# The free-axis differences of a grid update: from turned matmuls to shifted sums on GpSimd and VectorE

## The chip, the cores and the metric

The kernel runs on one core of a Trainium2 chip. The core has a matrix engine (TensorE, PE in the profile, with its weight loads as PEld), a vector engine (VectorE, DVE), a scalar engine (ScalarE, ACT), GpSimd (POOL) and SyncE (SP), which here only issues DMAs. Each engine works through its own queue of instructions in order and waits on semaphores for the others. The metric is the device time of one execution in microseconds (us); less is better. Times shown are medians of several runs, and a profile is one further execution.

## What is computed

Sixteen samples of 256 x 256 go through four layers: an adapter with a layer norm, an attention block of 16 heads with a feed-forward part, a branch that is chosen per sample and has a layer norm, and at last one explicit step of a differential equation on the 256 x 256 field. The change is in the last layer:

```
def _L3_cond_ref(f, A_grid, B_grid, dt):
    def _grad(f, axis):
        fm = jnp.moveaxis(f, axis, -1)
        g = (jnp.roll(fm, -1, -1) - jnp.roll(fm, 1, -1)) * 0.5
        g0 = (-3.0 * fm[..., 0] + 4.0 * fm[..., 1] - fm[..., 2]) * 0.5
        gN = (3.0 * fm[..., -1] - 4.0 * fm[..., -2] + fm[..., -3]) * 0.5
        ...
    def _grad2(f, axis):
        g = jnp.roll(fm, -1, -1) - 2.0 * fm + jnp.roll(fm, 1, -1)
        g0 = 2.0 * fm[..., 0] - 5.0 * fm[..., 1] + 4.0 * fm[..., 2] - fm[..., 3]
        gN = 2.0 * fm[..., -1] - 5.0 * fm[..., -2] + 4.0 * fm[..., -3] - fm[..., -4]
        ...
    Af = A_grid[None] * f[:, None]
    Bf = B_grid[None] * f[:, None]
    gradv_Af = _grad(Af[:, 0], 1) + _grad(Af[:, 1], 2)
    gradvv_Bf = _grad2(Bf[:, 0], 1) + _grad2(Bf[:, 1], 2) + _grad(_grad(Bf[:, 2], 2), 1) + _grad(_grad(Bf[:, 2], 1), 2)
    df = -gradv_Af + gradvv_Bf * 0.5
    f_new = f + df * dt[:, None, None]
    return jnp.maximum(f_new, 0.0)
```

Axis 1 of a sample lies on the partitions (two chunks of 128), axis 2 is the free axis. With G for the first difference and H for half the second one, the update is G (b2 f G' - a0 f) + H (b0 f) + (H' on b1 f and -G' on a1 f along the free axis), where the primed ones work along axis 2 and a0, a1, b0, b1, b2 are the grids. G and H have one-sided rows at both ends.

## The kernel before

All four layers of all samples are in flight at once. Each stage is a Python generator, a chain: `adapt`, `prepare`, `project`, `weigh`, `attend`, `divide`, `enter`, `feed`, `end`, `step`. The class `Flow` puts the chains in an order when the program is built: it keeps a clock for each engine, adds a written-down cost for each piece of work (`flow.pe`, `flow.dve`, `flow.act`, `flow.pool`, `flow.dma`), and at each turn goes on with a chain that could start on PE by now, the one with the smallest priority number first. A `yield at` says from when a chain can go on, `yield at, 0` that it needs no PSUM bank, and a third element `True` that it goes ahead of the others. The priority of each chain starts at the first number in `flow.add(...)` and grows by the PE time it has used over the second. The order that comes out is fixed, and on the chip semaphores alone hold it together. Some choices hang on the clocks: `normalized` and `taken_up` take DVE or ACT for a layer norm's scaling and for a copy out of PSUM, and `feed` does so for its bias.

Attention takes 64 groups of four heads (`QUADS`, four per sample). For each, a side input of 1024 KB comes by SP (`load_side`, L332; three buffers), and a DMA issued from POOL (`add_mask`, L532) adds the mask to it in place. `weigh` emits this copy among its own instructions, by `MASK_FROM`, `MASK_BY` and POOL's clock. L841 on DVE then adds scores and side and takes the maximum, L852 on ACT makes the exponentials, four transposes (L479) turn them, `taken_up` (L487 on DVE, L489 on ACT) copies them to SBUF, and L908 multiplies them with the values. The layer norms' statistics go through four small POOL instructions each (L436 to L440).

`step` handles the last layer, one sample at a time. `normalized_affine` makes the field f (L448 or L453, then L471 and L472 on POOL). Then PE transposes f (tile e_t, four L479), and DVE makes three products of the turned field with turned grids (L1216: b2, a1, b1). POOL makes two products of f as it lies (L1220 b0, L1221 a0). PE forms b2 f G' in ps_z (L1228, L1229), DVE adds it to a0 (L1234). In ps_d, PE sums H and G along the partitions (L1246 for a chunk's own part, L1252 for the rows of the other chunk) and the free-axis differences of a1 and b1, which as turned fields are the stationary operands (L1262). One float32 matmul of the source stands as two instructions in the trace, and a transpose as one. DVE multiplies by dt and adds f (L1284), ACT takes the Relu (L1288), SP sends the result (L1290). `wide` gives the tiles of a step from eight buffers; a sample takes seven.

Of the kernel before, what the change touches and what calls it, by code (L numbers as in the profile page):

```python
# [98 lines left out]
class Flow:  # L99
# [63 lines left out]
    def run(self):  # L163
        while self.chains:
            open_ = [c for c in self.chains if c[4] is None or c[4]()]
            assert open_, "no chain can go on"
            now = self.clock["PE"] + 0.0774
# [19 lines left out]
def chain_kernel(ctx: ExitStack, tc: tile.TileContext, t: dict, out: bass.AP):  # L187
# [136 lines left out]
    sides, side_at, masked = {}, {}, {}  # L324
# [64 lines left out]
    def load_mask(b):  # L389
        m8s[b] = wp.tile([P, NC, S], U8, name=f"m8_{b}", tag="m8", bufs=1)  # L390
        nc.sync.dma_start(out=m8s[b], in_=t["mask"][b])
        if b:
            flow.dma(0.3)
# [13 lines left out]
    def later(name, src, shape, cost):  # L407
# [8 lines left out]
        later("rows_b", rows(t["rows_b"]), [P, 3 * D + B], 1.2),  # L416
# [6 lines left out]
    dt = rows_b[:, 3 * D :]  # L423
    w1_sr, w2_sr = w_sr[:, :NC, :], w_sr[:, NC:, :]
    a0_g, a1_g, b0_g, b1_g, b2_g, g_m, h_m = (grids[:, :, i * S : (i + 1) * S] for i in range(7))
# [17 lines left out]
    def normalized(dst, src, stat, first=False):  # L443
        mv, rs, nb = stat

        if first or max(flow.clock["DVE"], flow.clock["POOL"]) <= flow.clock["ACT"] - 0.2509:
            for c in range(NC):
                nc.vector.tensor_scalar(  # L448
                    dst[:, c, :], src[:, c, :], mv[:, c, 0:1], rs[:, c : c + 1], ALU.subtract, ALU.mult
                )  # L450
            return flow.dve(0.65, flow.clock["POOL"])
# [32 lines left out]
    def taken_up(dst, ps, after):  # L484

        if flow.clock["DVE"] + 0.9485 <= flow.clock["ACT"]:
            nc.vector.tensor_copy(dst, ps)  # L487
            return flow.dve(0.6, after)
# [165 lines left out]
    def project():  # L654
        for b in range(B):
# [6 lines left out]
            at = transposed(ps_t, ln)  # L662
            done.add(("turned", b))
# [117 lines left out]
    MASK_FROM, MASK_BY = 2, 1  # L781

    def weigh():

        at = 0.0
        for m, (b, half, par) in enumerate(QUADS):
# [43 lines left out]
            done.add(("scores", m))  # L830
            if masked[m] > flow.clock["DVE"]:
                yield max(at, masked[m]), 0
            for i in range(4):
# [32 lines left out]
                to = m + 2 if i >= MASK_FROM else m + 1  # L866
                if 4 <= to < len(QUADS) and to not in masked:
                    if to % 4 == 0 and to // 4 not in negs:
                        spread_mask(to // 4)
                    if to == m + 1 and i == MASK_BY or flow.clock["POOL"] > side_at[to]:  # L870
                        masked[to] = add_mask(to)
# [12 lines left out]
    def attend():  # L884
        for m, (b, half, par) in enumerate(QUADS):
            if m % 4 == 0:
                yield lambda: ("values", b) in done
            for i in range(4):
# [5 lines left out]
                at = transposed(ps_p, pr)  # L894
                p_t = hp.tile([P, NC, S], F32, name=f"c_pts{n}", tag="c_pts", bufs=4)
# [25 lines left out]
    def divide(b, half):  # L921
# [10 lines left out]
        for c in range(NC):  # L932
            nc.tensor.transpose(ps_r[:, c, :], spread[:, c].rearrange("p h d -> p (h d)"), ident)
        over = hp.tile([P, S], F32, name=f"c_over{b}_{half}", tag="c_over", bufs=1)
        nc.scalar.copy(over, ps_r.rearrange("p c q -> p (c q)"))
        at = free(f"c_r{b}_{half}", flow.act(0.29, flow.pe(0.22)))
# [36 lines left out]
    def enter():  # L973
        for b in range(B):
# [9 lines left out]
            at = transposed(ps_t, ln)  # L984
            h_t = hp.tile([P, NC, S], F32, name=f"d_ht{b}", tag="d_ht", bufs=2)
# [10 lines left out]
    def feed():  # L996
        for b in range(B):
# [6 lines left out]
            for j in range(NF // 2):  # L1004
# [16 lines left out]
                on_act = flow.clock["DVE"] > flow.clock["ACT"] - 0.4406  # L1021
# [79 lines left out]
    reach = [slice(0, P + 1), slice(P - 1, S)]  # L1101

    def end():
# [3 lines left out]
        for b in range(B):  # L1107
# [7 lines left out]
            at = transposed(ps_t, y)  # L1115
            x_t = wide(f"d_xt{b}")
# [64 lines left out]

    def step():
# [5 lines left out]
        def awake(*columns):  # L1188

            ps = misc("awake", [P, NC * S])  # L1190
            for n in columns:
                nc.tensor.matmul(ps[:, :n], ident, b2_g[:, 0, :n], start=True, stop=True)
            free("awake", flow.clock["PE"])

        yield lambda: ("branch", 0) in done
        for g in (a0_g, a1_g):
            nc.gpsimd.tensor_scalar(g, g, -1.0, None, ALU.mult)
        for b in range(B):
            yield lambda: ("branch", b) in done
            if b < B - 1:  # L1200
# [3 lines left out]
                yield at  # L1204
# [4 lines left out]
            at_f = at  # L1209
            ps_t = misc(f"e_t{b}", [P, NC, S])  # L1210
            at = transposed(ps_t, f)
            if b == B - 1:
                awake(256, 256)
            b2_, a1, b1_ = (wide(f"e_{n}{b}") for n in ("b2", "a1", "b1"))
            for dst, grid in ((b2_, b2_g), (a1, a1_g), (b1_, b1_g)):
                nc.vector.tensor_tensor(dst, ps_t, grid, ALU.mult)  # L1216
                at = flow.dve(0.6, at)
            free(f"e_t{b}", at)
            a0, b0 = wide(f"e_a0{b}"), wide(f"e_b0{b}")
            nc.gpsimd.tensor_tensor(b0, f, b0_g, ALU.mult)  # L1220
            nc.gpsimd.tensor_tensor(a0, f, a0_g, ALU.mult)  # L1221
            at_b = flow.pool(1.25, at_f)
            at_0 = flow.pool(1.25)
            yield at - 1.4
            ps_z = misc(f"e_z{b}", [P, NC, S])
            for c in range(NC):
                rng = slice(c * P, (c + 1) * P)
                nc.tensor.matmul(ps_z[:, c, :], b2_[:, 0, rng], g_m[:, 0, :], start=True, stop=False)  # L1228
                nc.tensor.matmul(  # L1229
                    ps_z[:, c, reach[1]], b2_[:, 1, rng], g_m[:, 1, reach[1]], start=False, stop=True  # L1230
                )
            at = flow.pe(1.39)
            yield at, 0, True
            nc.vector.tensor_tensor(a0, ps_z, a0, ALU.add)  # L1234
            at_z = free(f"e_z{b}", flow.dve(0.61, max(at, at_0)))
            yield at_b
            if b == B - 2:
                yield lambda: ("branch", B - 1) in done
            o = wide(f"e_o{b}")
            ps_d = misc(f"e_d{b}", [P, NC, S])  # L1240


# [15 lines left out]
            for c in range(NC):  # L1258
                rng = slice(c * P, (c + 1) * P)
                for k in range(NC):  # L1260
                    for src, w in ((a1, g_m), (b1_, h_m)):
                        nc.tensor.matmul(  # L1262
                            ps_d[:, c, reach[k]],
                            src[:, k, rng],
                            w[:, k, reach[k]],
                            start=False,
                            stop=False,
                        )
            flow.pe(2.74)
            yield at_z  # L1270
            for w, src in ((h_m, b0), (g_m, a0)):
                for c in range(NC):
                    next_to(w, src, c)
# [3 lines left out]
            yield at, 0, True  # L1277
# [5 lines left out]
            for part in [slice(c, c + 1) for c in range(NC)] if b == B - 1 else [slice(0, NC)]:  # L1283
                nc.vector.scalar_tensor_tensor(  # L1284
                    o[:, part, :], ps_d[:, part, :], dt[:, b : b + 1], f[:, part, :], ALU.mult, ALU.add
                )
                at = flow.dve(0.34 if b == B - 1 else 0.68, at)
                nc.scalar.activation(o[:, part, :], o[:, part, :], AF.Relu)  # L1288
                flow.dma(0.4 if b == B - 1 else 0.8, flow.act(0.54, at))
                nc.sync.dma_start(out=out[b].rearrange("(c p) d -> p c d", p=P)[:, part, :], in_=o[:, part, :])  # L1290
# [3 lines left out]
    flow.add(adapt(), -1.707, 2.551)  # L1294
    flow.add(prepare(), -2.177, 3.484)
    flow.add(project(), 1.419, 9.878)
    flow.add(weigh(), -3.911, 108.6)
    flow.add(attend(), 0.9418, 11.1)
    flow.add(enter(), -11.15, 0.3324)
    flow.add(feed(), 2.331, 13.51)  # L1300
    flow.add(end(), 12.69, 2.249)
    flow.add(step(), 2.08, 4.955)
    flow.run()

def _arrays(inputs):
# [28 lines left out]
    g, h = _stencils()  # L1334
    a_grid, b_grid = l3["A_grid"], l3["B_grid"]
# [55 lines left out]
```

## Time and profile before

| what | value |
|---|---|
| median of 3 runs | 889.37 us (887.1 to 889.7) |
| the profiled execution | 894.71 us |
| its span, first to last instruction | 892.5 us |
| mean granted clock of PE | 0.983 |
| DMA, mean share of 16 engines | 74%, 209 GB/s |
| last chain of waits, start to end | 871.0 to 889.6 us, nearly all PE work of the last two steps |
| side copies by SP, issue to landing, median | 6.3 us (63 of 1024 KB) |
| mask copies by POOL, issue to landing, median | 8.6 us (60) |

The profile gives for each engine the time in which it was busy. A busy PE is not always a full one: matmuls overlap, and the recorded time of one is longer than the distance to the next. In rows of groups the columns are line, engine, operation, output and inputs, shape and count, then busy time in us and the mean in ns, then idle time just before and what ended it. In a timeline the columns are start and duration in us, engine, line, operation, tiles, shape and count; consecutive like instructions are merged. In rows of stretches, each engine's busy time is followed by the count of its instructions, then come the granted PE clock, the DMA share and GB/s.

### The profile page before, as it was taken

What the parts mean: (1) busy time and instruction counts of PE and PEld (TensorE: products, weight loads), DVE (VectorE), ACT (ScalarE), POOL (GpSimd) and SP (SyncE); (2) the same over time, 40 slices, a digit from 0 to 9 for tenths busy, and PEclk for the clock granted to TensorE, in tenths of its full rate; (3) what the DMA queues carried; (4) which work ended last, traced back from release to release, by engine and by line L of the source; (5) the groups of instructions that cost most, each with busy time, mean ns of one, the idle gap of its engine ahead of it and who ended that gap; (6) DMA issues with size and microseconds to landing.
All of it is one profiled execution on the core that took longest, in us unless ns stands there. A gap on an engine that the chain in (4) does not pass through costs nothing. (4 is left out here: it accounts for less than half of the span.)

```text
span 892.5 us, 18369 instructions
## 1 busy us (share of the span) xinstructions
PE 844.9 (95%) x6188; PEld 663.9 (74%) x6188; DVE 598.5 (67%) x2034; ACT 572.5 (64%) x1616; POOL 377.9 (42%) x516
## 2 busy tenths in 40 slices
PE   7888999999999999899999999999998999999997
PEld 3565777777868777777778878777877778777875
DVE  5775977767666867666687768657757566665434
ACT  2686769678574867657477577658675665775320
POOL 3445653843544528154271625151513416131543
PEclk8998999999999999999899999999999999999999
DMA  7979999879776897967769696977786876940111
GB/s 274 363 226 275 231 308 264 230 207 276 200 221 168 252 248 187 265 157 223 203 183 268 165 311 206 257 200 220 225 215 198 226 204 184 270 108 13 59 43 36
DMA packets 79244, 186.84 MB, mean 209 GB/s; under 512 B 8473, under 2 KB 22699, under 8 KB 71083
## 3 DMA queue, kind: packets, MB, share of 16 engines
q1 hardware_dynamic: 46192, 120.51, 39.4%
q0 software_dynamic: 31680, 62.92, 33.1%
q10 hardware_dynamic: 1275, 2.19, 0.7%
q8 instruction: 52, 0.85, 0.4%
q14 instruction: 45, 0.37, 0.1%
HBM read 94.89 MB, written 4.19 MB: 111 GB/s over the span
## 5 line engine op out<-in xcount | busy, mean ns | idle before, releaser
L852 ACT ACTIVATE c_pr<-c_pr,c_mx 128x256 f32<-128x256 f32 x512 | 254.8, 500 | 97.8 <-DVE c_mx L841 96.5
L841 DVE CUSTOM_DVE_ANT_0 c_pr<-c_s,side 128x256 f32<-128x256 f32 x512 | 191.1, 417 | 47.9 <-PE c_pt L479 17.1
L479 PE MATMUL c_pt<-ident,c_pr 128*128 128x128 f32 x1024 | 144.6, 282 | 10.4 <-DVE c_mx L841 5.6
L479 PEld LDWEIGHTS c_pt<-ident,c_pr 128*128 128x128 f32 x1024 | 117.0, 143 | 39.3 <-issue 12.4
L532 POOL DMA_DIRECT2D side<-neg x60 | 80.1, 1342 | 127.7 <-DVE c_mx L841 74.0
L436 POOL TENSOR_SCALAR rs<-mv 128x2 f32<-128x2 f32 x64 | 14.2, 222 | 275.5 <-DVE mv L433 274.8
L1010 PE MATMUL d_f<-d_ht,w 128*128 128x256 f32 x512 | 125.8, 390 | 1.0 <-DVE c_mx L841 0.5
L1042 PE MATMUL d_o<-w,d_z 128*128 128x256 f32 x512 | 121.4, 382 | 0.3
L487 DVE COPY c_pts<-c_pt 128x512 f32<-128x512 f32 x124 | 84.0, 685 | 40.2 <-PE c_pt L479 38.3
L1010 PEld LDWEIGHTS d_f<-d_ht,w 128*128 128x128 f32 x512 | 95.9, 195 | 16.7 <-issue 2.4
L1042 PEld LDWEIGHTS d_o<-w,d_z 128*128 128x128 f32 x512 | 94.4, 191 | 13.9 <-issue 1.3
L489 ACT COPY c_pts<-c_pt 128x512 f32<-128x512 f32 x132 | 74.4, 574 | 40.5 <-PE c_pt L479 39.9
L852 ACT ACTIVATION_READ_ACCUMULATOR c_pr<-c_pr,c_mx 128x1 f32 x512 | 96.7, 189 | 0.0
L908 PE MATMUL c_c<-c_pts,c_va 128*32 128x256 f32 x1024 | 72.2, 385 | 3.4 <-DVE c_cts L940 2.9
L822 PE MATMUL c_s<-c_st 32*128 32x256 f32 x960 | 47.7, 305 | 6.4 <-PEq L1146 2.9
L822 PEld LDWEIGHTS c_s<-c_st 32*128 32x128 f32 x960 | 34.4, 185 | 25.4 <-issue 13.0
L908 PEld LDWEIGHTS c_c<-c_pts,c_va 128*32 128x32 f32 x1024 | 27.8, 109 | 31.6 <-issue 11.0
L1034 DVE SCALAR_TENSOR_TENSOR d_z<-d_f,d_z 128x512 f32<-128x512 f32 x64 | 43.5, 680 | 10.9 <-ACT d_f L1030 9.0
L437 POOL TENSOR_TENSOR rs<-rs,inv_sqrt 128x2 f32<-128x2 f32 x64 | 45.8, 716 | 5.3
L1030 ACT ACTIVATE d_f<-d_z 128x512 f32<-128x512 f32 x64 | 38.4, 601 | 12.4 <-DVE d_z L1027 10.8
L1027 DVE TENSOR_SCALAR d_z<-d_f,cols 128x256 f32<-128x256 f32 x82 | 35.7, 477 | 14.7 <-PE d_f L1010 14.2
L841 DVE DVE_READ_ACCUMULATOR2_ANT c_mx<- 128x1 f32 x512 | 42.5, 83 | 0.0
(166 smaller groups left out, 1522.6 us busy)
## 6 DMA issues: line engine op xcount, KB each, us to landing
side<-in_side SPq DMA_DIRECT2D x63, 1024.0 KB, 6.3
side<-neg POOLq DMA_DIRECT2D x60, 1024.0 KB, 8.6
c_st<-c_qk SPq DMA_DIRECT2D x60, 192.0 KB, 5.4
d_w<-in_W_branch SPq DMA_DIRECT2D x16, 512.0 KB, 5.7
c_st<-c_qk SPq DMA_DIRECT2D x60, 128.0 KB, 5.5
xt<-in_x_t SPq DMA_DIRECT2D x16, 256.0 KB, 7.2
x<-in_x SPq DMA_DIRECT2D x16, 256.0 KB, 4.8
c_st<-c_qk SPq DMA_DIRECT2D x60, 64.0 KB, 5.3
```

Of the source, the lines that this page charges most:

```text
L437: nc.gpsimd.tensor_tensor(rs, rs, inv_sqrt, ALU.pow)
L479: nc.tensor.transpose(ps[:, k, c * P : (c + 1) * P], src[:, c, k * P : (k + 1) * P], ident)
L487: nc.vector.tensor_copy(dst, ps)
L489: nc.scalar.copy(dst, ps)
L532: nc.gpsimd.dma_start(out=sides[m].rearrange("p (h c) k -> p h (c k)", h=HB), in_=negs[m // 4].rearrange("p c k -> p (c k)").unsqueeze(1). ...
L822: nc.tensor.matmul(ps[i][:, c, :], stacked[rows32, par, 0, c * P : (c + 1) * P], stacked[rows32, par, part, :], start=part == 1, stop=part ...
L841: nc.vector.tensor_tensor_reduce(out=pr[:, c, :], in0=ps[i][:, c, :], in1=sb[:, i * NC + c, :], scale=-1.0, scalar=3.0e38, op0=ALU.add, op ...
L852: nc.scalar.activation(pr[:, c, :], pr[:, c, :], AF.Exp, bias=mx[:, c : c + 1], scale=-1.0, accum_out=sums[:, c, h : h + 1],)
L908: nc.tensor.matmul(ps_c[32 * i : 32 * i + 32, :], va[:, k, 4 * half + i, 2 * par : 2 * par + 2, :].rearrange("p e d -> p (e d)"), turned[i ...
L1010: nc.tensor.matmul(ps_f[:, i, :], w1[:, k, f * P : (f + 1) * P], h_t[:, k, :], start=k == 0, stop=k == NC - 1,)
L1034: nc.vector.scalar_tensor_tensor(z, ps_f, 1.0, z, ALU.add, ALU.mult)
L1042: nc.tensor.matmul(ps_o, us[f // 2][:, f % 2, c * P : (c + 1) * P], w2[:, f, :], start=f == 0, stop=f == NF - 1,)
```

## The change

The free-axis differences are no longer made with a turned field. The transposes, ps_z and the sixteen L1262 instructions go. Five products are made of f as it lies: w = b2 f, a0, b0, p and q, where the grids for p and q are prepared once on POOL (p_g becomes half the difference of the two loaded grids, q_g half their sum, w_g half the b2 grid). Interior columns come from sums of tiles shifted by one column: r from p and q, and a0 gets w of the right neighbour and loses w of the left one. The two outer columns come from small products of the outer four columns with prepared edge coefficients. For samples 0 to 14, w is made on DVE and a0, b0, p, q and the three sums of r on POOL; for sample 15, w, a0 and the three sums are on DVE and b0, p, q on POOL. The output then is (ps_d + r) dt + f, in r's own buffer. ps_d keeps only the partition-axis parts.

```diff
+    def shifted(engine, clock, cost, r, p, q, at):
+        mid, left, right = (slice(i, i + S - 2) for i in (1, 0, 2))
+        engine.tensor_tensor(r[:, :, mid], p[:, :, right], p[:, :, mid], ALU.subtract)
+        engine.tensor_tensor(r[:, :, mid], r[:, :, mid], q[:, :, left], ALU.add)
+        engine.tensor_tensor(r[:, :, mid], r[:, :, mid], q[:, :, mid], ALU.subtract)
+        return clock(3 * cost, at)
...
-        yield lambda: ("branch", 0) in done
-        for g in (a0_g, a1_g):
-            nc.gpsimd.tensor_scalar(g, g, -1.0, None, ALU.mult)
+        yield lambda: ("finish", 0) in done
+        edge_r, edge_z, edge_t = (fixed(f"edge_{n}", edge) for n in "rzt")
+        for dst, grid, i in ((edge_r, p_g, 0), (edge_t, q_g, 1), (edge_z, w_g, 2)):
...
+            nc.gpsimd.tensor_tensor(dst, ends(grid), of.unsqueeze(1).to_broadcast(edge), ALU.mult)
+        nc.gpsimd.tensor_tensor(edge_r, edge_r, edge_t, ALU.add)
+        nc.gpsimd.tensor_scalar(a0_g, a0_g, -1.0, None, ALU.mult)
...
+        nc.gpsimd.tensor_tensor(diff, q_g, p_g, ALU.subtract)
+        nc.gpsimd.tensor_tensor(q_g, q_g, p_g, ALU.add)
+        nc.gpsimd.tensor_scalar(p_g, diff, 0.5, None, ALU.mult)
+        for g in (q_g, w_g):
+            nc.gpsimd.tensor_scalar(g, g, 0.5, None, ALU.mult)
...
-            ps_t = misc(f"e_t{b}", [P, NC, S])
-            at = transposed(ps_t, f)
-            for dst, grid in ((b2_, b2_g), (a1, a1_g), (b1_, b1_g)):
-                nc.vector.tensor_tensor(dst, ps_t, grid, ALU.mult)
-            nc.gpsimd.tensor_tensor(b0, f, b0_g, ALU.mult)
-            nc.gpsimd.tensor_tensor(a0, f, a0_g, ALU.mult)
-            ps_z = misc(f"e_z{b}", [P, NC, S])
...
-            nc.vector.tensor_tensor(a0, ps_z, a0, ALU.add)
+            if end_:
+                nc.vector.tensor_tensor(w, f, w_g, ALU.mult)
+                nc.vector.tensor_tensor(a0, f, a0_g, ALU.mult)
+                made = ((b0, b0_g), (p, p_g), (q, q_g))
+            else:
+                nc.vector.tensor_tensor(w, f, w_g, ALU.mult)
+                made = ((a0, a0_g), (b0, b0_g), (p, p_g), (q, q_g))
+            for dst, grid in made:
+                nc.gpsimd.tensor_tensor(dst, f, grid, ALU.mult)
+            if not end_:
+                at_r = shifted(nc.gpsimd, flow.pool, 1.25, r, p, q, at_q)
+            nc.vector.tensor_tensor(a0[:, :, mid], a0[:, :, mid], w[:, :, right], ALU.add)
+            nc.vector.tensor_tensor(a0[:, :, mid], a0[:, :, mid], w[:, :, left], ALU.subtract)
+            for i, g in enumerate((edge_z, edge_r)):
+                nc.vector.tensor_tensor(prod[:, i], ends(f), g, ALU.mult)
+            nc.vector.tensor_tensor(half, prod[:, :, :, :, 0:2], prod[:, :, :, :, 2:4], ALU.add)
+            for i, dst in enumerate((a0, r)):
+                nc.vector.tensor_tensor(outer(dst), half[:, i, :, :, 0], half[:, i, :, :, 1], ALU.add)
+            if end_:
+                at_r = shifted(nc.vector, flow.dve, 0.6, r, p, q, at_q)
...
-                    for src, w in ((a1, g_m), (b1_, h_m)):
-                        nc.tensor.matmul(ps_d[:, c, reach[k]], src[:, k, rng], w[:, k, reach[k]], ...)
...
-                nc.vector.scalar_tensor_tensor(o[...], ps_d[...], dt[:, b : b + 1], f[...], ALU.mult, ALU.add)
+                nc.vector.tensor_tensor(o, ps_d[:, part, :], o, ALU.add)
+                nc.vector.scalar_tensor_tensor(o, o, dt[:, b : b + 1], f[:, part, :], ALU.mult, ALU.add)
```

The host side gives the grids unturned and adds 24 numbers (the one-sided coefficients) to rows_b.

The rest of the change is in the plan. The mask copies get a chain of their own, in place of the lines in `weigh`:

```diff
+    def mask():
+        for m in range(4, len(QUADS)):
+            yield lambda: m in sides
+            if m % 4 == 0:
+                yield m8_at[m // 4], 0
+                spread_mask(m // 4)
+            yield side_at[m], 0, True
+            masked[m] = add_mask(m)
...
+            yield lambda: m in masked
```

After the transposes in `project`, `attend`, `enter` and `end`, and around the copies in `divide`, a `yield at, 0, True` is added, so that the copy out of PSUM is put in its place (and on its engine) only when the plan's clock has come to it. The plan's numbers are others: the allowance in `Flow.run` (0.0774 to 0.04507), the three thresholds of the engine choices (0.2509 to 0.354, 0.9485 to 0.5659, 0.4406 to 0.3293), and the start and rate of every chain.

## The prediction

> **What bounds the kernel now.** I read the page's first part for the engines' shares, then the busy time by stretches of the span, then the groups of instructions kept apart by shape, and last the timeline of a stretch without attention, to see whether a busy PE is a full one.
>
> ```profile
> PE 844.9 (95%) x6188; PEld 663.9 (74%) x6188; DVE 598.5 (67%) x2034; ACT 572.5 (64%) x1616; POOL 377.9 (42%) x516
> ```
>
> ```profile
> 89.00:178.00 89.00, 84.06 (x657) 65.28 (x656) 73.46 (x262) 66.82 (x202) 51.99 (x71) 1.00 0.93 260
> 803.00:848.00 45.00, 44.55 (x282) 37.23 (x277) 22.65 (x58) 20.52 (x49) 16.21 (x25) 1.00 0.11 36
> ```
>
> ```profile
> 808.29 0.60 PE L1228 MATMUL e_z<-grids,e_b 128*128 128x256 f32 x2
> 808.72 0.39 PE L1229 MATMUL e_z<-grids,e_b 128*128 128x129 f32 x2
> 808.95 0.60 PE L479 MATMUL c_pt<-ident,c_pr 128*128 128x128 f32 x4
> ...
> 810.25 0.39 PE L1262 MATMUL e_d<-grids,e_a 128*128 128x129 f32 x2
> 810.47 0.39 PE L1262 MATMUL e_d<-grids,e_b 128*128 128x129 f32 x2
> ```
>
> PE is busy for 844.9 of 892.5 us, so it idles for 47.6. From 803 to 848, with 11% DMA and DVE half idle, it is busy for 44.55 of 45.00 us, and the starts show that this is a full queue: two L1262 follow two others after 0.22 us, two 256-wide L1228 take 0.43, two L1229 0.23. So there one instruction costs 0.11 us (128 or 129 columns) or 0.215 (256), and its recorded 0.27 to 0.40 is overlap. From 89 to 178 the other engines are at their fullest (DVE 73.46 of 89, 83%; DMA 0.93) and PE still has 84.06. Every group of PE instructions, at the pitch of its starts (median), adds up to about 825 us. PE is the bound in nearly all stretches but the first 45 us and the last 20.
>
> [...]
>
> **What is removed on PE.** Per sample four transposes (0.44 us at 0.11), four 256-wide and four 129-wide instructions of ps_z (0.86 and 0.44), and sixteen L1262 (1.76): 28 instructions, 3.50 us, and 56.0 for 16 samples. They stand inside the full stream, so all of it counts. Two PSUM tiles per sample fall away too; an easier choice of bank may close holes, which I bound by 0 to 5 us and take as 0.
>
> **What moves to POOL.** Before, a sample has two multiplications there.
>
> ```profile
> L1220 POOL TENSOR_TENSOR e_b<-y,grids 128x512 f32<-128x512 f32 x16 | 22.9, 1428 | 1.3 <-DVE y L465 1.0
> L471 POOL TENSOR_TENSOR e_tmp<-e_tmp,rows_b 128x512 f32<-128x512 f32 x15 | 19.5, 1300 | 14.4 <-DVE e_tmp L448 13.6 <-ACT e_tmp L453 0.8
> ```
>
> After, samples 0 to 14 have four multiplications and three shifted sums, sample 15 three multiplications: 108 - 32 = 76 more, at 1.27 (the fastest of this size in the timeline) to 1.43: 97 to 109 us, taken 103. The preparation of the grids grows to about 10 us (four scalings at 1.56, two wide sums at 1.35, six small ones near 0.2), 7 more than now. POOL goes from 378 to 488. In the built instruction list it is a burst of seven, 7 x 1.27 = 8.9 us, and what queues behind it are the statistics of other samples (L436 to L440), for which ACT or DVE normalise and PE then transposes, and mask copies.
>
> **What DVE gets.** Out go three L1216 (0.685 each) and L1234 (0.69), 2.74 us. In come w (0.69), two 254-wide sums into a0 (0.68 each), five edge instructions (0.17 to 0.24 by the 128x16 rows at the start of the kernel, 0.2 taken) and the sum of ps_d and r (0.69 like L1234): 3.74. That is 1.0 per sample and 2.7 more for the last, whose a0 and shifts are on DVE: 19 us. The new plan also gives copies to other engines (built lists: c_pts on DVE 124 to 154, at 0.685; c_ln 24 to 14, d_z 82 to 72, d_ln 10 to 16, d_xt 4 to 6, e_tmp 26 to 24): DVE +14, ACT about -8 with two more table loads of 1.283. DVE stands at 631, ACT at 564. At a span near 848 that is 74% and 67%, under the 83% beside which PE stayed at 94%: the cover is DVE's idle time, and gone above 83%.
>
> **The new contact of DVE and POOL.** Nine of the new DVE instructions per sample (w, two sums, five edges, the last multiply-add) read only SBUF. The trace has few such rows; nearest are the normalisations L448, which read SBUF alone.
>
> ```profile
> 633.90 0.73 DVE L448 TENSOR_SCALAR e_tmp<-y,mv,rs 128x256 f32<-128x256 f32 x2
> ```
>
> ```profile
> 97.97 1.69 DVE L448 TENSOR_SCALAR c_ln<-x,mv,rs 128x256 f32<-128x256 f32 x2
> ```
>
> ```profile
> 97.40 1.77 POOL L544 TENSOR_TENSOR x<-x,rows_a 128x512 f32<-128x512 f32 x1
> ```
>
> A pair takes 0.73 alone and 1.69 here, ending soon after POOL's wide instruction; over the timeline the 12 pairs that overlap wide POOL work take 1.17 in the mean, 1.82 at most, the others 0.75. PSUM readers show nothing (L487 0.686 and 0.687). So one instruction pays 0 to 1.1 us, 0.21 in the mean, which I take: 9 x 15 x 0.21 = 28 us more DVE busy time, 659 or 78%, still covered. For its delay to others and for statistics behind the burst I put 6 us on the path, bounds 0 and 30.
>
> [...]
>
> **The rest.** Preparing the grids: 10 us of POOL behind sample 0's statistics, near 75 us, covered by PE work of samples 1 and 2; 2 us taken, bounds 0 and 10. The end: in the built PE list sample 15's feed-forward has little of other samples between its parts, so PE waits about 2.1 us for the last gate (0.84 + 0.60 + 0.69), 1.5 for the turned copy, 2.1 for the branch's Gelu with its table. Against this, L1174 no longer starts 2.3 us after its matmuls, behind sample 14's products. I take +4, bounds -2 and +8. Sample 15's own step stays near 10 us: two products, two sums and edges 3.8, shifts 2.05, then adds and Relu near 2.2, behind 1.4 for sample 14's output. rows_b grows from 392 to 404 KB, 0.06 us at 209 GB/s, under the early side loads. The mask chain issues the same 60 copies and 16 spreads at other places in POOL's queue; the late copies change order alone. Both are in the 6 us, with the mask's own risk below.
>
> **Sum.** 892.5 - 56.0 + 6 + 2 + 4 = 848.5 span. The profiled execution took 894.71, 2.2 around its span, so 850.7; the median shown, 889.37, is 0.6% below that execution (x 0.994): 845.5, said as 845.
>
> **Rivals.** First, late masks.
>
> ```profile
> DVE c_pr L841 <- DMA side<-neg: 8.7, 3, 5.8
> ```
>
> DVE waits for a mask three times now. Issue of L532 plus its median 8.6 us to landing, against the first L841 of each quad, leaves slacks of -0.4 to 18.5 us, 38 of 60 below a burst's 8.9. In the built list 12 bursts still have mask copies behind them. If each pushes one back by its 8.9 us, the mean lateness over these slacks is 2.15: 26 us, 874.5 span, 876.7 with what lies around it, median 871. For it: POOL's queue is in order. Against: only 6 of the 60 copies stand directly behind a burst, and PE has other chains to run.
>
> Second, the slower side: DVE becomes the bound through POOL's bursts. The place is the nine SBUF instructions of a step, the price 1.1 us each: 9 x 15 x 1.1 = 149, DVE 631 + 149 = 780, and at 82.5% fill the span is 945, median 942. It is slower than before from DVE 736 on (0.825 x 892.5), or 0.78 us an instruction. For it: bursts and these instructions belong to the same sample. Against: overlapping pairs pay 0.21.
>
> Third, no change: PE's place in the queue is taken by waits already there, and 889 stays. The full stretch from 803 to 848 speaks against it.
>
> Fourth, the full gain and closed holes: 892.5 - 61 = 831.5, median 829 or less.
>
> **Chances.** The forecast (828 to 862) 0.66, late masks 0.14, DVE bound 0.07, no change 0.03, better than 828 0.10. The range 826 to 868 takes the first, about half of the last and half of the masks: 0.78 to 0.80. A difference of 0.3% is about what the measurement can tell from none: faster 0.90, same 0.03, slower 0.07.
>
> **What would show it.** PE busy near 789 with 448 fewer instructions, idle near 60; DVE 645 to 675; POOL near 490, its new wide sums at 1.3 to 1.45; DVE's 254-wide sums near 0.9 where they meet POOL. Mask waits of DVE above 30 us would show the first rival, DVE above 730 the second. I am wrong if PE idles for over 80 us, or if idle falls below 45.

## The result and the profile after

The changed kernel takes 938.63 us (936.89 to 942.14, four runs), against 888.24 us (885.52 to 889.70) for the kernel before on the same chip: a ratio of 1.0576, interval 1.0533 to 1.0619. Forecast were 845 us, with 0.07 for a slower kernel. The profiled execution has a span of 935.9 us and a mean granted clock of 0.927, against 892.5 and 0.983.

The page's first part, and from its slices the row of the granted clock, for the kernel after:

```profile
PE 828.3 (89%) x5740; PEld 620.8 (66%) x5740; DVE 697.1 (74%) x2135; ACT 566.2 (60%) x1602; POOL 492.3 (53%) x602
...
PEclk8999999999899998997997989998899979899886
```

The 448 PE instructions are gone (5740 against 6188), and POOL has 492.3 us where 488 was worked out. Yet PE's busy time fell by 16.6 us only, and it idles for 107.6 us (935.9 - 828.3) instead of 47.6. The forecast had 789 busy and about 60 idle, so 39 us of the 87 by which the span missed are instructions that ran longer, and 48 are idle time. The granted clock says why they ran longer: 13 of the 40 slices lie below 0.9. In steps of 2.5 us, the time with a granted clock under 0.75 is 133 us; before it was 35. PE's busy time in each of these steps, times the part of the clock that is missing there, adds up to 50 us, and before to 14: the difference of 36 us is nearly all of the 39.

The list of waits, first for the kernel after, then before. A row has who waited, for whom, us in total, how often, and the longest; rows of other waits stand between these.

```profile
ACT c_pr L861 <- DVE c_mx L850: 161.8, 106, 11.9
...
PEld e_d L1296 <- DVE e_a L1279: 25.1, 10, 5.4
DVE e_r L1279 <- POOL e_r L1194: 21.1, 9, 2.5
```

```profile
ACT c_pr L852 <- DVE c_mx L841: 96.5, 89, 4.0
```

ACT's exponentials wait 65 us longer for the maxima that DVE takes, and the longest wait has gone from 4.0 to 11.9 us. L850 itself is as fast as before (416 ns). So it starts late, behind something in DVE's queue. The groups of the step on DVE by line and shape, kernel after, show behind what; then two of POOL:

```profile
L1273 DVE TENSOR_TENSOR e_a<-e_a,e_w 128x508 f32<-128x508 f32 x16 | 30.9, 1930 | 8.7 <-POOL e_a L1266 8.5
L1261 DVE TENSOR_TENSOR e_w<-y,grids 128x512 f32<-128x512 f32 x15 | 28.3, 1889 | 5.5 <-POOL y L471 5.5
L1274 DVE TENSOR_TENSOR e_a<-e_a,e_w 128x508 f32<-128x508 f32 x16 | 23.3, 1455 | 0.6
L1276 DVE TENSOR_TENSOR e_ed<-y,edge_z 128x16 f32<-128x16 f32 x16 | 15.2, 949 | 0.0
L1317 DVE SCALAR_TENSOR_TENSOR e_r<-e_r,rows_b,y 128x512 f32<-128x512 f32 x15 | 11.8, 785 | 0.5
L1277 DVE TENSOR_TENSOR e_eh<-e_ed 128x16 f32<-128x16 f32 x16 | 10.2, 637 | 0.6
L1316 DVE TENSOR_TENSOR e_r<-e_d,e_r 128x512 f32<-128x512 f32 x15 | 10.1, 677 | 7.6 <-PE e_d L1290 7.6
```

```profile
L1266 POOL TENSOR_TENSOR e_p<-y,grids 128x512 f32<-128x512 f32 x16 | 27.6, 1726 | 0.0
L1266 POOL TENSOR_TENSOR e_q<-y,grids 128x512 f32<-128x512 f32 x16 | 27.4, 1713 | 0.0
```

L1316, which reads PSUM, has the expected 0.68 us. Five of the rows that read only SBUF (w, the two sums into a0, the first edge product L1276, the edge sum L1277) have two to six times their own time, a 16-column product 0.95 us in the mean. The means hide the shape: the fifteen products w took 0.66 to 1.50 us twelve times and 4.79, 5.61 and 6.88 us three times. The timeline of the longest:

```profile
480.06 1.34 POOL L531 DMA_DIRECT2D side<-neg  x1
...
480.95 1.75 POOL L1266 TENSOR_TENSOR e_a<-y,grids 128x512 f32<-128x512 f32 x1
481.01 6.88 DVE L1261 TENSOR_TENSOR e_w<-y,grids 128x512 f32<-128x512 f32 x1
482.20 1.73 POOL L1266 TENSOR_TENSOR e_b<-y,grids 128x512 f32<-128x512 f32 x1
483.42 1.72 POOL L1266 TENSOR_TENSOR e_p<-y,grids 128x512 f32<-128x512 f32 x1
484.64 1.71 POOL L1266 TENSOR_TENSOR e_q<-y,grids 128x512 f32<-128x512 f32 x1
485.86 1.48 POOL L1192 TENSOR_TENSOR e_r<-e_p 128x508 f32<-128x508 f32 x1
487.41 1.60 POOL L1193 TENSOR_TENSOR e_r<-e_r,e_q 128x508 f32<-128x508 f32 x1
...
488.09 0.40 ACT L933 COPY c_spr<-c_rec 128x256 f32<-128x256 f32 x1 [6.17 <-DVE c_rec L931]
...
488.90 0.66 PE L937 MATMUL c_r<-ident,c_spr 128*128 128x128 f32 x2 [5.29 <-DVE c_qk L732]
```

POOL's product begins 0.06 us ahead of DVE's. The next POOL instructions start every 1.22 us although each is recorded with 1.7: five in a row follow without a pause. The first pause comes when the fifth ends (485.86 + 1.48 = 487.34), as L1193 needs its result; w ends at 487.89, 0.55 us later, a little less than its own 0.66 us. Nothing else runs on DVE in this time; ACT then has waited 6.17 us and PE 5.29. Not every burst holds DVE for so long. In another one of this kernel the same products are in the queue, and DVE gets in between them:

```profile
236.29 1.26 POOL L1266 TENSOR_TENSOR e_b<-y,grids 128x512 f32<-128x512 f32 x1
236.35 1.74 DVE L1273 TENSOR_TENSOR e_a<-e_a,e_w 128x508 f32<-128x508 f32 x1 [0.64 <-POOL e_a L1266]
237.51 1.71 POOL L1266 TENSOR_TENSOR e_p<-y,grids 128x512 f32<-128x512 f32 x1
238.13 1.64 DVE L1274 TENSOR_TENSOR e_a<-e_a,e_w 128x508 f32<-128x508 f32 x1
239.19 1.70 POOL L1266 TENSOR_TENSOR e_q<-y,grids 128x512 f32<-128x512 f32 x1
```

The sum waits for the product that is running, about 1.1 us, and POOL's q starts 1.68 us after p instead of 1.22. What tells the two kinds apart is what POOL did just before. Six of the fifteen bursts start 0.9 us after POOL issued a mask copy (L531, at 480.06 above). In these six all four products are recorded with 1.71 to 1.79 us and start 1.22 to 1.25 us apart, and there lie all five instructions of the step that took over 2 us: the three long w and two sums of 5.16 us. In the nine other bursts no instruction paid more than about 1.1 us. Why a burst behind a mask copy lets nothing in is not shown, and no run moved the mask copies away.

The stretch of the long w in busy times per 5 us (PE, PEld, DVE, ACT, POOL, each with its count, then the granted clock, DMA share and GB/s):

```profile
480.00:485.00 5.00, 3.61 (x40) 2.33 (x32) 4.68 (x5) 1.92 (x7) 5.00 (x6) 1.00 0.98 270
485.00:490.00 5.00, 1.10 (x5) 0.80 (x6) 5.00 (x9) 1.28 (x4) 4.84 (x5) 0.88 0.40 100
490.00:495.00 5.00, 3.41 (x11) 2.10 (x9) 4.90 (x15) 1.48 (x6) 3.08 (x3) 0.50 0.87 228
495.00:500.00 5.00, 5.00 (x18) 2.94 (x18) 1.85 (x8) 2.03 (x8) 0.00 (x0) 0.50 1.04 288
```

PE runs dry, and after that its granted clock is 0.50 for 10 us. What that makes of the same work, four transposes, before the burst and after it:

```profile
475.12 0.60 PE L478 MATMUL d_t<-ident,y 128*128 128x128 f32 x4
...
499.01 1.06 PE L478 MATMUL c_pt<-ident,c_pr 128*128 128x128 f32 x4
```

The clock of 0.50 came after the 5.29 us in which PE stood still; how short a gap brings it is not shown.

### The profile page after: what moved, and what is told of

Read it like the earlier page. It is cut to its first block, busy times and chain, and to the rows that moved or that the text cites. A ratio compares the mean times of both kernels' runs of the same rounds, so it can differ in the third digit from the quotient of the medians.

```text
span 935.9 us, 17580 instructions
## 1 busy us (share of the span) xinstructions
PE 828.3 (89%) x5740; PEld 620.8 (66%) x5740; DVE 697.1 (74%) x2135; ACT 566.2 (60%) x1602; POOL 492.3 (53%) x602
## 5 line engine op out<-in xcount | busy, mean ns | idle before, releaser
L861 ACT ACTIVATE c_pr<-c_pr,c_mx 128x256 f32<-128x256 f32 x512 | 255.0, 499 | 163.1 <-DVE c_mx L850 161.8
L850 DVE CUSTOM_DVE_ANT_0 c_pr<-c_s,side 128x256 f32<-128x256 f32 x512 | 192.5, 416 | 26.2 <-PE c_s L830 8.9
L478 PE MATMUL c_pt<-ident,c_pr 128*128 128x128 f32 x1024 | 161.2, 285 | 7.7 <-DVE c_mx L850 2.0
L478 PEld LDWEIGHTS c_pt<-ident,c_pr 128*128 128x128 f32 x1024 | 119.1, 144 | 52.5 <-issue 20.9
L531 POOL DMA_DIRECT2D side<-neg x60 | 80.3, 1346 | 89.9 <-DMA side<-in_side 30.1
L1017 PE MATMUL d_f<-d_ht,w 128*128 128x256 f32 x512 | 123.2, 385 | 4.7 <-ACT d_ht L994 2.5
L486 DVE COPY c_pts<-c_pt 128x512 f32<-128x512 f32 x154 | 104.9, 684 | 29.5 <-PE c_pt L478 28.4
L1017 PEld LDWEIGHTS d_f<-d_ht,w 128*128 128x128 f32 x512 | 93.6, 192 | 18.2 <-ACT d_ht L994 2.9
L912 PE MATMUL c_c<-c_pts,c_va 128*32 128x256 f32 x1024 | 75.8, 395 | 10.0 <-DVE c_pts L486 5.7
L488 ACT COPY c_pts<-c_pt 128x512 f32<-128x512 f32 x102 | 57.8, 575 | 19.5 <-PE c_pt L478 18.7
L912 PEld LDWEIGHTS c_c<-c_pts,c_va 128*32 128x32 f32 x1024 | 28.7, 110 | 43.4 <-issue 16.6
L830 PE MATMUL c_s<-c_st 32*128 32x256 f32 x960 | 49.6, 311 | 2.0 <-DVE c_pts L486 1.0
L850 DVE DVE_READ_ACCUMULATOR2_ANT c_mx<- 128x1 f32 x512 | 42.3, 83 | 0.0
L1034 DVE TENSOR_SCALAR d_z<-d_f,cols 128x256 f32<-128x256 f32 x72 | 31.4, 478 | 9.7 <-PE d_f L1017 9.5
```

The source lines that it names most:

```text
L478: nc.tensor.transpose(ps[:, k, c * P : (c + 1) * P], src[:, c, k * P : (k + 1) * P], ident)
L488: nc.scalar.copy(dst, ps)
L531: nc.gpsimd.dma_start(out=sides[m].rearrange("p (h c) k -> p h (c k)", h=HB), in_=negs[m // 4].rearrange("p c k -> p (c k)").unsqueeze(1). ...
L830: nc.tensor.matmul(ps[i][:, c, :], stacked[rows32, par, 0, c * P : (c + 1) * P], stacked[rows32, par, part, :], start=part == 1, stop=part ...
L850: nc.vector.tensor_tensor_reduce(out=pr[:, c, :], in0=ps[i][:, c, :], in1=sb[:, i * NC + c, :], scale=-1.0, scalar=3.0e38, op0=ALU.add, op ...
L861: nc.scalar.activation(pr[:, c, :], pr[:, c, :], AF.Exp, bias=mx[:, c : c + 1], scale=-1.0, accum_out=sums[:, c, h : h + 1],)
```

## The experiments

Theories. A: a DVE instruction that reads only SBUF is held while POOL's burst reads SBUF, DVE's queue stops behind it, PE idles and its clock falls. B: the plan's changes do it. C: the burst's length does it, as masks and statistics queue behind it on POOL. D: DVE's queue stands still in order, in front of an instruction that needs POOL's result.

**1. The plan alone.** Against the changed kernel, as all diffs here but those of runs 9 and 11, which name theirs: the step of the kernel before, with the mask chain, the late copies, the allowance and the thresholds of the change; the chains' starts and rates are those of before.

```diff
-        yield lambda: ("finish", 0) in done
-        edge_r, edge_z, edge_t = (fixed(f"edge_{n}", edge) for n in "rzt")
...
+            ps_t = misc(f"e_t{b}", [P, NC, S])
+            at = transposed(ps_t, f)
...
-    flow.add(step(), 0.9776, 1.725)
+    flow.add(step(), 2.08, 4.955)
```

> The step of before (turned field) under the new plan's mask chain, late copies and thresholds, with the old rates of the chains. Theory A (DVE instructions that read only SBUF are held by POOL's burst, stop DVE's queue, PE idles and its clock falls): 880 to 900 us, PE clock 0.97 or more. Theory B (the plan's changes cost the time): 920 or more.

899.91 us, ratio 1.0112 (1.0082 to 1.0143), clock 0.982. This part of the plan costs about 1% on the old step, far from the 920 us of B. The chains' new starts and rates are not in it; run 2 has the new step without any of the plan.

**2. The new step alone**, under the whole plan of before.

```diff
-            now = self.clock["PE"] + 0.04507
+            now = self.clock["PE"] + 0.0774
...
-            yield lambda: m in masked
...
+                    if to == m + 1 and i == MASK_BY or flow.clock["POOL"] > side_at[to]:
+                        masked[to] = add_mask(to)
...
-    flow.add(step(), 0.9776, 1.725)
+    flow.add(step(), 2.08, 4.955)
```

> The new step under the whole old plan. Theory A: 920 to 955 us, clock near 0.93, the w product on DVE again up to several us long. Theory B: 830 to 860, since the step alone saves 56 us of PE work.

981.93 us, 1.1005 (1.0895 to 1.1115), clock 0.92; w has a mean of 1.61 us, the two sums 1.82 and 1.54, and ACT waits 174 us for the maxima. More than either theory gave, and with run 1 it rules B out as the cause: with the new step, the new plan is worth some 43 us (981.9 - 938.6).

**3. DVE's part behind the burst.**

```diff
-                nc.vector.tensor_tensor(w, f, w_g, ALU.mult)
-                at_w = flow.dve(0.6, at)
...
                 at_r = shifted(nc.gpsimd, flow.pool, 1.25, r, p, q, at_q)
+                yield at_r + 2.0, 0
+                nc.vector.tensor_tensor(w, f, w_g, ALU.mult)
+                at_w = flow.dve(0.6)
```

> The changed kernel, but for samples 0 to 14 the DVE part of a step is put into the plan after POOL's seven instructions by the plan's clock. Theory A: DVE's w near 0.7 us in most samples, clock 0.96 or more, 850 to 890 us. Theory C (POOL's burst itself holds masks and statistics back): stays at 925 to 945, since POOL's work is the same. Theory B: stays too.

892.63 us, 1.0042 (1.002 to 1.0064), clock 0.962. POOL's burst has the same work, and 46 us have come back, so the burst by itself doesn't explain most of the loss. But DVE now waits 25.9 us for masks (9 times, longest 6.9; in the kernel after 2.0): C has a part once the hold is mostly gone. w has a mean of 1.01 us, with one still at 3.8: the plan's clock only roughly meets the end of the burst. The time lies just above A's range.

**4. All of it on POOL.** w, the two sums and the edges are emitted on POOL too; DVE keeps the last two instructions.

```diff
-                nc.vector.tensor_tensor(w, f, w_g, ALU.mult)
...
-                made = ((a0, a0_g), (b0, b0_g), (p, p_g), (q, q_g))
+                made = ((w, w_g), (a0, a0_g), (b0, b0_g), (p, p_g), (q, q_g))
...
+            eng = nc.vector if end_ else nc.gpsimd
-            nc.vector.tensor_tensor(a0[:, :, mid], a0[:, :, mid], w[:, :, right], ALU.add)
+            eng.tensor_tensor(a0[:, :, mid], a0[:, :, mid], w[:, :, right], ALU.add)
...
```

> The changed kernel, but for samples 0 to 14 POOL also makes w, the two sums into a0 and the five edge instructions, so that the step has no SBUF-only product or sum on DVE but the last multiply-add; POOL's burst grows from 7 wide instructions to 10 and 5 small ones. Theory A: 845 to 885 us, clock 0.96 or more, DVE busy near 590. Theory C: slower than the changed kernel, 940 to 970. Theory B: 930 to 950.

871.14 us, 0.9763 (0.9665 to 0.9861), clock 0.982: POOL does more (544.5 us), its burst is longer, and the kernel is faster than before. C gave 940 to 970 here, so the burst's length is not what costs the most. DVE now waits 24.4 us for masks, 12 times, longest 3.5: the first rival's effect, near the size it was given (26 us), but, as in run 3, not in the kernel that was forecast.

**5. Only the wait for r away.** DVE's small instruction on r's outer columns, the only one in the step's first part that needs the whole burst, goes behind the PE part.

```diff
-            for i, dst in enumerate((a0, r)):
-                nc.vector.tensor_tensor(outer(dst), half[:, i, :, :, 0], half[:, i, :, :, 1], ALU.add)
+            nc.vector.tensor_tensor(outer(a0), half[:, 0, :, :, 0], half[:, 0, :, :, 1], ALU.add)
...
             yield max(at, at_r), 0, True
...
+            nc.vector.tensor_tensor(outer(r), half[:, 1, :, :, 0], half[:, 1, :, :, 1], ALU.add)
```

> The changed kernel with one DVE instruction moved: the outer columns of r, which wait for POOL's last sum, come after PE's part of the step instead of before it. Theory A (POOL's burst keeps DVE's SBUF-only instructions out): a small gain, 915 to 935 us, w and the sums into a0 on DVE as long as before. Theory D (DVE's queue stops because it waits in order for POOL's results): 850 to 895.

923.34 us, 1.0382 (1.0298 to 1.0466), clock 0.941; w and the sums are as long as before the edit (1.87, 1.94, 1.46 us). D by itself is worth 15 us while the instructions are still held.

**6. A POOL that only writes.** The seven POOL instructions become memsets of the same tiles.

```diff
-                nc.gpsimd.tensor_tensor(dst, f, grid, ALU.mult)
+                if end_:
+                    nc.gpsimd.tensor_tensor(dst, f, grid, ALU.mult)
+                else:
+                    nc.gpsimd.memset(dst, 0.0)
...
-                at_r = shifted(nc.gpsimd, flow.pool, 1.25, r, p, q, at_q)
+                for _ in range(3):
+                    nc.gpsimd.memset(r[:, :, mid], 0.0)
+                at_r = flow.pool(3.75, at_q)
```

> The changed kernel, but for samples 0 to 14 POOL's seven wide instructions are memsets of the same tiles, so a0, b0, p, q and r are left out of the computation; DVE's part is unchanged. Theory A in the form that POOL must read SBUF to keep DVE out: DVE's w and sums at 0.66 to 0.70 us in every sample, clock 0.97 or more, 840 to 870. If any POOL work beside them slows them, w has cases of 2 us and more and the time stays above 890.

838.13 us, 0.9424 (0.9349 to 0.9499), clock 0.988. The groups of DVE, this kernel:

```profile
L1261 DVE TENSOR_TENSOR e_w<-y,grids 128x512 f32<-128x512 f32 x15 | 12.1, 805 | 7.0 <-POOL y L471 7.0
L1278 DVE TENSOR_TENSOR e_a<-e_a,e_w 128x508 f32<-128x508 f32 x16 | 10.9, 681 | 4.6 <-POOL e_a L1269 4.4
L1279 DVE TENSOR_TENSOR e_a<-e_a,e_w 128x508 f32<-128x508 f32 x16 | 11.0, 688 | 0.6
```

w has a median of 0.69 us and takes 1.51 at most, where it took 6.88; the two sums have their own 0.68 and 0.69 in the mean. The four memsets of the products overlap here (in one burst a start every 0.46 us, recorded with 1.03 each) without a pause; where the first sum waits, it is for the first of them (4.4 us in all), so it runs beside the others, and is not held. But a burst of memsets, first start to last end, is 3.7 us where the real one is 9.8, so two things were changed at once.

**7. Extra work for PE.** Eight unused 256-wide matmuls behind each w, 240 instructions in the trace, at the 0.215 us of the full stream 52 us of work.

```diff
                 at_w = flow.dve(0.6, at)
+                awake(256, 256, 256, 256, 256, 256, 256, 256)
```

> The changed kernel with eight more 256-wide matmuls without use put into PE's queue behind each w product of samples 0 to 14: 16 instructions at 0.215 us, 3.4 us a sample, 52 in all. Theory A with PE standing still there and losing its clock: they lie in PE's holes, the mean clock rises above 0.94, and the time is 915 to 950, far less than 52 more. If PE's stream were still full, 980 to 995.

933.70 us, 1.0499 (1.0414 to 1.0583); the clock rises from 0.927 to 0.962 and the time under 0.75 falls from 133 to 76 us. 52 us more work cost nothing: PE had holes of that size, and filling them raised the clock.

**8. All on POOL, mended.** As run 4, with sample 15's products all on DVE, a step back to the plan between products and sums, and the last two instructions through PSUM, so that no DVE instruction of a step reads two SBUF tiles next to its own burst on POOL.

```diff
-                nc.vector.tensor_tensor(o, ps_d[:, part, :], o, ALU.add)
-                nc.vector.scalar_tensor_tensor(o, o, dt[:, b : b + 1], f[:, part, :], ALU.mult, ALU.add)
+                nc.vector.tensor_tensor(ps_d[:, part, :], ps_d[:, part, :], o, ALU.add)
+                nc.vector.scalar_tensor_tensor(o, ps_d[:, part, :], dt[:, b : b + 1], f[:, part, :], ALU.mult, ALU.add)
```

> The kernel with the whole step on POOL, and three edits: the last multiply-add reads its sum from PSUM instead of SBUF, sample 15's products are all on DVE, and the plan may put other POOL work between products and sums. Theory A: the last multiply-add of samples 0 to 14 falls from 1.04 to 0.75 us, sample 15's w and a0 products from 1.75 to 0.7, 855 to 872 us. Without the contact mattering: 871 as it was.

866.32 us, 0.9748 (0.968 to 0.9816), clock 0.984, the lowest median here of a kernel that computes everything. Its interval overlaps that of run 4, so the time doesn't tell the two apart. The rows do: the last multiply-add fell from 1.04 us in run 4 to 0.75, the two products of sample 15 from 1.75 to 0.68.

**9. Memsets, as many as needed for a long burst.** Each memset of run 6 twice: bursts of 7.8 us.

```diff
-                    nc.gpsimd.memset(dst, 0.0)
+                    nc.gpsimd.memset(dst, 1.0)
+                    nc.gpsimd.memset(dst, 0.0)
...
-                for _ in range(3):
+                for _ in range(6):
```

> The memset kernel with each memset issued twice, so that POOL's burst is about as long as the products and sums it stands for (14 memsets of 0.6 to 0.73 us, some 8 to 9 us); a0, b0, p, q and r are again left out of the computation. Theory A (reading is what keeps DVE out): DVE's w at 0.69 us where it was 4.8 to 6.9, 835 to 850 us. If the length of POOL's burst is what matters: w of 2 us and more again, above 880.

898.58 us, 1.0118 (1.0053 to 1.0183), clock 0.955: 60 us more than run 6, far from what A gave. Groups and waits of this kernel:

```profile
L1261 DVE TENSOR_TENSOR e_w<-y,grids 128x512 f32<-128x512 f32 x15 | 12.0, 798 | 3.6 <-POOL y L471 3.6
```

```profile
ACT c_pr L861 <- DVE c_mx L850: 146.8, 106, 9.9
DVE e_r L1285 <- POOL e_r L1276: 54.5, 15, 4.5
```

Next to the memsets the two sums take 0.68 and 0.69 us in the mean, the first edge product 0.17, and w has a median of 0.69 and takes 1.49 at most: the hold goes with POOL's products and sums, which read SBUF, and not with the length of the burst. Whether their reading or something else in them does it no run takes apart. (The second memset of a tile starts 0.06 us after the first has ended, so these bursts have short pauses; the overlapping memsets of run 6 have none, and the sums were not held there either.) The length costs time all the same: DVE stands 54.5 us in front of the small instruction on r, 15 times, with the maxima behind it. In the kernel after the same wait showed only 21.1 us, since DVE arrived there late, from being held.

**10. Pauses in the burst.** A tiny POOL instruction that needs the product just made, behind each product.

```diff
                 nc.gpsimd.tensor_tensor(dst, f, grid, ALU.mult)
+                if not end_:
+                    nc.gpsimd.tensor_scalar(dst[:, 0, 0:2], dst[:, 0, 0:2], 1.0, None, ALU.mult)
```

> The changed kernel with a small POOL instruction behind each of the four products that scales two columns of its result by one, so that POOL pauses for its own results between the products; 4 x 0.22 us more POOL work a sample. Theory A in the form that POOL's products follow one another without a pause and DVE gets in only at a pause: DVE's longest w falls from 6.9 to below 3.5 us, 895 to 925 us. If a waiting DVE instruction has to wait for the whole burst whatever its pauses: longest w 7 us or more, 935 to 950.

958.90 us, 1.0797 (1.0731 to 1.0863), clock 0.917. The longest w is 2.26 us instead of 6.88: with pauses DVE gets in, as A says of w. A's time, 895 to 925 us, is missed by far, though: bursts are 11.1 us long now, the wait for r is 55.2 us, and the edge instructions are still held (1.02 and 0.92 us in the mean). Getting in earlier moves DVE to the next wait.

**11. All on POOL, products apart.** Run 8 with a return to the plan after every product.

```diff
                 ats.append(flow.dve(0.6, at) if end_ else flow.pool(1.25, at))
+                if not end_:
+                    yield flow.clock["POOL"] - 0.6, 0
```

> The step on POOL as in the last version of it, with the plan free to put other POOL work between any two of the five products (each waits until the plan's POOL queue is nearly empty). If masks and statistics behind the burst are what is left of the loss, DVE's waits for masks fall from 24 us to below 10 and the time to 845 to 862; if not, 863 to 870.

884.26 us, 0.9944 (0.9915 to 0.9974), clock 0.965, slower than either range. DVE's mask waits fell from 24.1 to 10.4 us, but PE's loads of the step now wait 15.4 us for a0 and 12.2 for b0. With other work between POOL's products the step itself comes late; that this is what costs the 18 us is argued from these waits, not tested.

**12. Both away.** Run 9's memsets and run 5's move together.

```diff
+                    nc.gpsimd.memset(dst, 1.0)
+                    nc.gpsimd.memset(dst, 0.0)
...
+            nc.vector.tensor_tensor(outer(a0), half[:, 0, :, :, 0], half[:, 0, :, :, 1], ALU.add)
...
+            nc.vector.tensor_tensor(outer(r), half[:, 1, :, :, 0], half[:, 1, :, :, 1], ALU.add)
```

> The changed kernel with GpSimd's seven instructions per sample replaced by memsets, each given twice (the burst is as long as with the real work, a0, b0, p, q and r are left out as in e9_write_long), and with DVE's small instruction on r's outer columns moved behind the step's PE part as in e5_edge_late. e9 took 898.58 us; DVE stood 54.5 us in front of that instruction, until GpSimd had finished r. If this wait in order (D) is what is left of the loss once the held instructions are gone, the time comes down to what e6_write_only took, 835 to 855 us, with that wait under 15 us and the granted clock above 0.975. If the length of the burst costs time by itself (C: masks, statistics and a0 come late whatever DVE does), the time stays at 885 to 900, and the masks' or statistics' waits of DVE and ACT are what has grown against e6.

848.74 us, 0.9543 (0.9506 to 0.9579), clock 0.975. The page's first part and the waits of this kernel:

```profile
PE 790.3 (93%) x5740; PEld 601.6 (71%) x5740; DVE 630.8 (75%) x2135; ACT 566.6 (67%) x1602; POOL 458.0 (54%) x707
```

```profile
ACT c_pr L861 <- DVE c_mx L850: 121.9, 106, 9.6
...
DVE e_r L1319 <- POOL e_r L1276: 2.3, 3, 1.7
```

The same bursts as in run 9, and 50 us less: the wait in order for r was most of what was left. The 10.6 us from here to run 6 go with the longer bursts and were not taken apart.

The two causes hide one another. From the kernel after, taking away the hold alone gives 40 us (run 9), taking away the wait alone 15 (run 5), both 90 (run 12). That fits the order of things on DVE: while an instruction is held, POOL goes on, and the wait that follows is the shorter for it (21.1 us in the kernel after, 54.5 in run 9). Two limits of this remain. The memset bursts are 2 us shorter than the real ones, so a part of the 90 us may be burst length. And they leave out part of the computation, so 848.74 us is no time that a complete kernel was shown to reach.

## Why the prediction was wrong

**The step that failed** is the new contact of DVE and POOL: "one instruction pays 0 to 1.1 us, 0.21 in the mean", "still covered", and "6 us on the path, bounds 0 and 30". It failed three times over.

The price: between the kernel after and run 12 the rows of w, the two sums, the first edge product and the edge sum differ by 16.5 + 20.0 + 12.3 + 12.5 + 7.4 = 68.7 us, not 28. The nearest rows were tensor_scalar instructions next to one or two wide POOL instructions; the bound of 1.1 us is the rest of one such instruction. As a bound for one instruction it held for most, but the mean of 0.21 did not: in a burst, several in a row pay nearly the whole of it. And five paid far more, in bursts right behind a mask copy (up to 6.2 us more than their own time, 24 of the 68.7 us together). How much of the lost time comes from these five and how much from the many short holds no run takes apart.

The cover: DVE's idle time was named as the cover, "gone above 83%". DVE is at 74%, and the cover was gone. What counts here is not how much of DVE is used but what stands behind the held instruction in its queue: L850's maxima, for which ACT waits 161.8 us instead of 96.5 (121.9 in run 12), and behind ACT the transposes on PE. DVE's idle time lay elsewhere in the span.

The wait: the sum had no term for the instruction on r's outer columns, which is queued on DVE in front of other samples' work and needs the last of seven POOL instructions. It was written as one of nine instructions that read SBUF, not as a wait. By runs 9 and 12 it is worth 50 us once the hold is gone.

To this the clock adds its part: 39 us of longer PE instructions, for which the sum had no term either. The prediction's own sign of being wrong, PE idle for over 80 us, came true with 107.6.

**The rivals.** Late masks: in the kernel after DVE waits 2.0 us for masks, once; the rival fell, and shows only where the hold is out of the way (25.9 us in run 3, 24.4 and 24.1 where POOL does everything, runs 4 and 8). DVE as the bound through POOL's bursts named the place and the sign, and its 942 us lie next to the 938.6. But its mechanism was DVE filled to 82.5%, with 0.78 us an instruction as the point from which it decides. Measured are 0.5 us (66.7 us of DVE busy time against run 6, over 135 instructions) and 74%. The number agrees by luck; the mechanism is blocking, not filling.

**What held.** PE's 28 instructions per sample: run 12 has 790.3 us of PE busy time (789 forecast) and 56.0 idle (about 60). The reading of PE as full before stands with it. POOL's 492.3 stands against 488, its shifted sums at 1.25 to 1.40 us. DVE without the contact has 630.8 in run 12, and 631 was worked out. With hold and wait away the span is 846.3 us, where the sum without its 6 us for the contact gives 842.5. So the rest of the sum was sound, with the reserve above on how run 12 differs from a complete kernel.

## What to carry to other kernels

Before work is split between DVE and GpSimd, list which DVE instructions read only SBUF while a GpSimd burst runs, and price each by the length of one GpSimd instruction (up to 1.1 us more here), and by the whole stretch up to the first pause where, as behind the mask copies here, the burst may let nothing in (up to 6.2 us more); then look at what stands behind it in DVE's queue, not at DVE's idle share. An instruction that needs the end of another engine's burst belongs, as run 12 against run 9 shows, where it is no longer waited for in front of other work. Moving everything onto the slower engine (its products start 1.22 us apart at best; DVE's own take 0.68), and letting DVE read one input from PSUM (the last multiply-add took 0.75 us instead of 1.04), gave 866.3 us here where sharing gave 938.6.

## What the runs showed of the hardware

- Next to POOL products of 128 x 512, DVE's sums of two SBUF tiles waited for the product that was running (1.74 us instead of 0.68). In bursts right behind a mask copy issued by POOL, where the products start 1.22 to 1.25 us apart and are recorded with 1.71 to 1.79 each, the three w (4.79, 5.61 and 6.88 us) and two sums (5.16) that came during them did not get in before the first pause for a dependent instruction. With such a pause behind each product, the longest w fell from 6.88 to 2.26 us.
- The wait went the other way too: in three samples w starts 0.04 or 0.05 us ahead of POOL's first product and takes 0.69 us, and POOL's second product starts 1.74 us after the first instead of 1.23.
- Next to memsets on POOL (0.52 to 0.73 us each in the mean in run 9) DVE's two sums kept their 0.68 and 0.69 us, in bursts of 3.7 us as of 7.8, and w had a median of 0.69.
- The hold fell on small instructions as on wide ones: a 16-column product took 0.95 us in the mean, and 0.17 next to the long bursts of memsets.
- After 5.29 us in which PE stood still, the granted clock was 0.50 for 10 us, and 0.75 for the next 5. Matmuls that nobody needs, put into such holes, raised the mean clock from 0.927 to 0.962 at no cost in time, though they did not make the kernel clearly faster: the intervals of the two ratios overlap.
